# Layer 1's output projection folded into the seven-product scheme, as a third stream beside q and k

## The chip, the cores and the metric

The kernel runs on one core of one Trainium2 chip. The metric is the time of one execution on the device in microseconds (us), the median of several runs. The engines are called as in the profile: PE is the matrix engine (PEld its weight loads), ACT the scalar engine, DVE the vector engine, POOL the GpSimd engine, SP the engine that issues most transfers.

## What is computed

Two attention layers run one after the other over x of shape 1 x 128 x 256 x 256: 128 rows, each of 256 tokens with 256 channels, all float32. Each layer normalizes its input over groups of 8 channels, attends within every row, and adds its result to its input. Layer 1 is what the change is about:

```python
x2 = x.reshape(B * T, F, C)
qkv = x2 @ w_in.T + b_in
...
scores = jnp.einsum('bhid,bhjd->bhij', q, k) / jnp.sqrt(jnp.asarray(D, x.dtype))
keep = jnp.abs(i - j) <= band
scores = jnp.where(keep, scores, -jnp.inf)
attn = jax.nn.softmax(scores, axis=-1)
out = jnp.einsum('bhij,bhjd->bhid', attn, v)
y = out @ w_out.T + b_out
```

with 4 heads of 64 channels and a band of 16. Layer 0 has 8 heads of 32 channels, a bias added after its softmax, and a gate.

## The kernel before

Data lies channel by token: a row is a tile of 128 partitions by 2 halves of the channels by 256 tokens. A first stage (about 170 us) makes layer 0's bias and statistics, layer 0 follows, and layer 1 begins at about 2087 us. Between the layers x is kept in device memory (`x1`), and layer 1 reads it back two rows at a time into `yg` tiles (`load1`, five buffers).

A projection of two rows by a 256 x 256 weight is eight products of a 128 x 128 block of weights by 256 tokens (one row, one half of the channels in, one half out). Both layers' q and k, and layer 0's v and gate, are made by seven such products for a pair of rows instead of eight, by a Strassen-like scheme. `Quarters` holds sums of weight blocks, `row_sums` makes four sums `ts` of the pair's normalized input `xn` on POOL, and `Seven` issues products 1 to 7 (`product`), copies partial results out of the accumulator bank on ACT (`take`: "15" after products 1 and 5, "6", "7", and "34" at the end), and adds the pieces on POOL (`add`, lines 618 and 619). `sevens` runs two such projections f and g against each other. Product 2 of both goes into a bank of its own (`twos`), so that a pair of projections takes three accumulator banks.

The output projection of layer 1 (`project`, `one_by_one`, line 662) is plain: four products per row, eight per pair. `sevens` interleaves some of them as `po` between q's and k's products.

Layer 1's main loop takes one pair of rows per turn, and a hand-written order (`manual_schedule`) fixes what PE, ACT, DVE and POOL each do, in the order of the calls. For turn s (rows s and s+1), before the change:

- `scores` of both rows (PE line 997, then ACT's exponentials at 1005, then on POOL the mask product 1007 and the fold `zp` at 1014);
- `attend` for the two rows of the turn before (PE lines 1029 and 1039), `total` (ACT 1051, copies the denominators z out and sums them);
- `project(s - 4)`, then on DVE `inverse` (the reciprocal, line 1057) and `divide` (1063) for the two rows, with `finish(s - 4)` (bias and residual, 1081, and two transposes, 1095) between them, then `least` (1069);
- `stretch`: q and k for the next pair by `sevens`, with `project(s - 3)` between the products; `finish(s - 3)` and `store` to the output;
- `normal` for the pair after the next (ACT 940, then `row_sums` on POOL, 566 to 569), and `values` (PE 976, ACT 983) for the next pair.

The accumulator banks of layer 1 are a ring of four one-bank tiles, shared by scores, projections and values, and two tiles of two banks for `avz`.

Of the kernel before, what the change touches and what calls it, by code (L numbers as in the profile page):

```python
# [9 lines left out]
F32 = mybir.dt.float32  # L10
# [29 lines left out]
def conv_preact_kernel(  # L40
# [108 lines left out]

    NS = ("s1", "s2", "s3", "s4", "n11")

    class Quarters:

# [6 lines left out]
            return self.source[:, kt, self.col + m * P : self.col + (m + 1) * P]  # L162

        def sum(self):
            s1, s2, s3, s4, n11 = (self.sums[:, n, :] for n in range(len(NS)))
            w00, w10, w01, w11 = (self.quarter(kt, m) for m in range(2) for kt in range(2))
            nc.gpsimd.tensor_tensor(s1, w01, w11, ALU.add)
            nc.gpsimd.tensor_tensor(s2, s1, w00, ALU.subtract)
            nc.gpsimd.tensor_tensor(s3, w00, w01, ALU.subtract)
            nc.gpsimd.tensor_tensor(s4, w10, s2, ALU.subtract)  # L170
            nc.gpsimd.tensor_scalar(n11, w11, -1.0, None, op0=ALU.mult)

        def stationary(self, n):

            if n <= 2:
                return self.quarter(n - 1, 0)
            return self.sums[:, NS.index({3: "s4", 4: "n11", 5: "s1", 6: "s2", 7: "s3"}[n]), :]

    quarters = {w: Quarters(const, qkv_sb, n * C, w) for n, w in enumerate("qkv")}
    quarters["g"] = Quarters(const, gate_sb, 0, "g")  # L180
# [380 lines left out]
                )  # L561
        return ps

    def row_sums(t, x):

        nc.gpsimd.tensor_tensor(t[:, 0], x[:, 2], x[:, 0], ALU.subtract)
        nc.gpsimd.tensor_tensor(t[:, 1], x[:, 3], t[:, 0], ALU.subtract)
        nc.gpsimd.tensor_tensor(t[:, 2], x[:, 3], x[:, 2], ALU.subtract)
        nc.gpsimd.tensor_tensor(t[:, 3], t[:, 1], x[:, 1], ALU.subtract)

    class Seven:


        def __init__(self, pool, weights, x, t, name, tag, by_token=False, bias=None):
            self.weights, self.x, self.t, self.name, self.by_token, self.bias = weights, x, t, name, by_token, bias
            self.to = pool.tile([P, 4, R], F32, tag=tag, name=name, bufs=2)
            self.mid = pool.tile([P, 2, R], F32, tag="mid", name=f"mid{name}", bufs=2)

        def open(self):
            self.ps = proj_bank(f"p{self.name}")  # L580
# [21 lines left out]
                nc.scalar.activation(to, ps, AF.Identity, bias=self.bias[:, half : half + 1])  # L602

        def take(self, what):
            if what == "15":
                nc.scalar.copy(self.to[:, 0:4:3, :], self.ps)
            elif what == "6":
                self.copy(self.mid[:, 0, :], self.ps[:, 0, :], 0)
            elif what == "7":
                self.copy(self.mid[:, 1, :], self.ps[:, 0, :], 1)  # L610
            elif self.bias is None:
                nc.scalar.copy(self.to[:, 1:3, :], self.ps)
            else:
                self.copy(self.to[:, 1, :], self.ps[:, 0, :], 1)
                nc.scalar.copy(self.to[:, 2, :], self.ps[:, 1, :])  # L615

        def add(self, two):
            nc.gpsimd.tensor_tensor(self.to[:, 0], self.to[:, 0], two, ALU.add)  # L618
            nc.gpsimd.tensor_tensor(self.to[:, 2:4], self.to[:, 2:4], self.mid, ALU.add)  # L619

    def sevens(pool, f, g, name, po, rest=lambda: None):


        for p in (f, g):
            p.open()
            p.product(1)
            p.product(5)
            p.take("15")
            if p is f:
                rest()  # L630
        twos = proj_bank(f"p2{name}")
        two = pool.tile([P, 2, R], F32, tag="two", name=f"two{name}", bufs=2)
        f.product(2, twos[:, 0, :], first=True)
        g.product(2, twos[:, 1, :])
        if f.bias is None:
            nc.scalar.copy(two, twos)  # L636
        else:
            f.copy(two[:, 0, :], twos[:, 0, :], 0)
            g.copy(two[:, 1, :], twos[:, 1, :], 0)
        for p in (f, g):  # L640
            p.product(3)
            p.product(6)
            p.take("6")

        for n, what in ((7, "7"), (4, "34")):
            f.product(n)
            f.take(what)
            next(po, None)
            g.product(n)
            g.take(what)  # L650
        for _ in po:
            pass
        for n, p in enumerate((f, g)):
            p.add(two[:, n, :])

    def one_by_one(w, at, name, done):

# [19 lines left out]
    with ExitStack() as both:  # L677
        st1 = both.enter_context(tc.tile_pool(name="st1", bufs=1))

        stats1 = st1.tile([P, 2, S // 2 + 1, 6], F32, name="stats1")  # L680
        quarters1 = {w: Quarters(st1, w_in_t, n * C, f"1{w}") for n, w in enumerate("qk")}
        big1 = both.enter_context(tc.tile_pool(name="big1", bufs=2))
        ygs = {}

        def load1(g):
            if g * XG < S and g not in ygs:
                yg = big1.tile([P, XG, 2, R], F32, tag="yg", name=f"yg{g}", bufs=5)
                nc.sync.dma_start(out=yg, in_=rows(x1, g * XG, XG))
                ygs[g] = yg

        with ExitStack() as lay0:
# [27 lines left out]
            def sum_rows(i):  # L719
                if 2 * i < S:  # L720
                    tss[i] = row.tile([P, 4, R], F32, tag="ts", name=f"ts{i}", bufs=1)
                    row_sums(tss[i], xns[i])

            def scores(s, half):
                i, r = divmod(s, 2)
# [106 lines left out]
            def stretch(names, i, s, rest=lambda: None):  # L832

                po = iter(())
                if s >= 0:
                    po = one_by_one(out_sb, st[s]["at"], f"po{s}", lambda ps: st[s].update(po=ps))
                if 2 * i >= S:
                    rest()
                    for _ in po:
                        pass  # L840
                    return
                f, g = (
                    Seven(row, quarters[w], xns[i], tss[i], f"{w}{i}", w, by_token=(w == "v")) for w in names
                )
                for w, p in zip(names, (f, g)):
                    res[w, i] = p.to
                sevens(row, f, g, f"{names}{i}", po, rest)


            with tc.manual_schedule(engines={mybir.EngineType.PE, mybir.EngineType.Activation, mybir.EngineType.DVE}):  # L850
# [67 lines left out]
        with ExitStack() as lay:  # L918
# [10 lines left out]
            def normal(i, by_scalar):  # L929
# [13 lines left out]
                                x, y, mean1[:, col], rstd1[:, col], op0=ALU.subtract, op1=ALU.mult  # L943
                            )
                tss[i] = row.tile([P, 4, R], F32, tag="ts", name=f"1ts{i}", bufs=2)
                row_sums(tss[i], xns[i])

            def project(s):

# [1 line left out]
                    return iter(())  # L951
                return one_by_one(w_out_t, st[s]["at"], f"1po{s}", lambda ps: st[s].update(po=ps))

            def stretch(i, po):

                if 2 * i >= S:
                    for _ in po:
                        pass
                    return
                f, g = (  # L960
                    Seven(row, quarters1[w], xns[i], tss[i], f"1{w}{i}", w, bias=bqk[:, 0:2] if w == "q" else None)
                    for w in "qk"
                )
                sevens(row, f, g, f"1qk{i}", po)
                for r in range(2):
                    st[2 * i + r].update(q=f.to[:, 2 * r : 2 * r + 2, :], k=g.to[:, 2 * r : 2 * r + 2, :])

# [91 lines left out]
            def divide(s):  # L1059
                if s < 0:  # L1060
                    return
                at = row.tile([P, 2, R], F32, tag="at", name=f"1at{s}")
                nc.vector.tensor_tensor(at, hd.pop(s)[:, :, 0, :], st[s]["rz"], ALU.mult)
                st[s]["at"] = at

# [5 lines left out]
            def add(s, by_vector):  # L1071
# [1 line left out]
                if s < 0:  # L1073
                    return
                po, y = st[s]["po"], ygs[s // XG][:, s % XG]
                ot = row.tile([P, 2, R], F32, tag="ot", name=f"1ot{s}")
                st[s]["ot"] = ot
                for half in range(2):
                    b = bo_v[:, half : half + 1]
# [24 lines left out]
                    for a in range(A):  # L1104
                        nc.sync.dma_start(out=in_strips(out[0], s - 1, 2, a), in_=o[strip(a)])

            def finish(s):
                add(s, True)

            load1(0)  # L1110
            with tc.manual_schedule(engines={
# [6 lines left out]
                values(1)  # L1118
                normal(1, False)
                nc.vector.scalar_tensor_tensor(shift1, mean1, -1.0, rstd1, op0=ALU.mult, op1=ALU.mult)  # L1120
                stretch(0, iter(()))
                for s in range(0, S + 2, 2):
                    if s < S:
                        scores(s)
                        scores(s + 1)
# [1 line left out]
                    attend(s - 1)  # L1127
                    total(s - 2)
                    total(s - 1)
                    for _ in project(s - 4):  # L1130
                        pass
                    inverse(s - 2)
                    if s < S - 2:
                        finish(s - 4)
                    divide(s - 2)
                    inverse(s - 1)
                    divide(s - 1)
                    if s < S - 2:
                        least(s - 2)
                        least(s - 1)  # L1140
                        stretch(s // 2 + 1, project(s - 3))
                        finish(s - 3)
                        store(s - 3)
                        normal(s // 2 + 2, True)
                        values(s + 2)
                        values(s + 3)
                    else:

                        for _ in project(s - 3):
                            pass  # L1150
                        add(s - 4, False)
                        add(s - 3, False)
                for s in (S - 2, S - 1):
# [9 lines left out]

                for s in (S - 6, S - 5):
                    turn_row(s)
                finish(S - 1)
                for s in (S - 2, S - 4, S - 3):
                    turn_row(s)
                store(S - 1)
# [200 lines left out]
```

## Time and profile before

| | |
|---|---|
| median of 3 runs | 3215.15 us (3213.65 to 3216.70) |
| profiled execution, its own time | 3215.86 us |
| its span, first to last instruction | 3214.2 us |
| mean granted clock of PE | 0.991 |
| PE busy over the span | 3131.4 us (97%) |
| DVE, ACT, POOL busy | 2656.1, 2014.7, 1691.9 us |
| layer 1, 2200 to 3100 us: PE, DVE, ACT, POOL busy of 900 us | 898.5, 644.0, 582.2, 677.2 us |
| one turn of layer 1's loop, from one pair's reciprocal to the next (2599.83, 2616.88) | 17.05 us |

In the timeline a row gives the start, the time, the engine, the line, the operation, output and inputs, the shape and the count of merged instructions, and in brackets the idle time before it and who ended it. A 256-column product appears as two matmul records. A record's duration contains its way through the pipeline, so the pace is read from start to start.

### The profile page before, as it was taken

To read this page: it belongs to the slowest core of one execution; us is meant where nothing else is said; L and a number is where in the kernel's file an instruction comes from. 1 tells how busy PE (TensorE), PEld (TensorE's weight loads), DVE (VectorE), ACT (ScalarE), POOL (GpSimd) and SP (SyncE) were. 2 spreads that over 40 slices of the span, in tenths; PEclk is the share of its full clock that TensorE was granted. 3 is DMA by queue.
4 is the path that set the end of the run, shared out by engine and by line. 5 is a ranking of instruction groups with operands and counts; after the bars stand their busy time and mean duration, and the time that the engine had idled before them with its cause. 6 is when DMAs were issued, how large, how long until landed. Compare 5 with 4: busy or idle time off the path is not lost.

```text
span 3214.2 us, 86812 instructions
## 1 busy us (share of the span) xinstructions
PE 3131.4 (97%) x36965; PEld 2454.8 (76%) x36965; DVE 2656.1 (83%) x3507; ACT 2014.7 (63%) x4316; POOL 1691.9 (53%) x1660
## 2 busy tenths in 40 slices
PE   6789999999999999999999999999999999999997
PEld 4567777777777777777777777678888888888886
DVE  4669999999999999999999999847677777777776
ACT  4656666666666666666666666466666666666664
POOL 3034444444444444444444444286777777777775
PEclk8989999999999999999999999999999999999998
DMA  9931211111111111111111111012222222222222
GB/s 376 423 102 54 54 34 41 34 41 34 41 34 41 34 41 34 41 34 41 34 41 34 41 34 34 21 28 54 67 62 60 68 67 54 67 68 61 61 68 48
DMA packets 346187, 209.38 MB, mean 65 GB/s; under 512 B 273592, under 2 KB 339136, under 8 KB 339648
## 3 DMA queue, kind: packets, MB, share of 16 engines
q1 hardware_dynamic: 344896, 201.37, 21.7%
q8 instruction: 293, 4.80, 0.6%
q0 software_dynamic: 752, 2.36, 0.2%
q14 instruction: 102, 0.84, 0.1%
q10 hardware_dynamic: 144, 0.00, 0.0%
HBM read 136.59 MB, written 67.11 MB: 63 GB/s over the span
## 4 chain that ended last, share of the span: by engine, by line
PE 92%; DMA 4%; DVE 3%; POOL 0%; issue 0%; ACT 0%; SPq 0%; DVEq 0%; ACTq 0%; POOLq 0%
PE sim L731 8%; PE p1v L976 7%; PE 1po L662 7%; PE po L662 7%; PE av L763 7%; PE bv L763 7%; PE pv L595 6%; PE pq L591 6%; PE p1q L591 5%; PE pk L591 5%; PE pg L591 5%; PE p1k L591 5%; PE zs L777 4%; PE 1sim L997 3%; PE 1avz L1029 2%; DMA pr<-in_L_conv_pair_repr_dram 2%
## 5 line engine op out<-in xcount | busy, mean ns | idle before, releaser
L744 ACT ACTIVATE ex<-sim 128x512 f32<-128x512 f32 x1024 | 547.6, 605 | 429.6 <-PE sim L731 429.6
L1057 DVE RECIPROCAL 1rz<-1z 128x512 f32<-128x512 f32 x128 | 427.8, 3342 | 315.0 <-ACT 1z L1051 315.0
L753 DVE TENSOR_TENSOR both<-ex 128x512 f32<-128x512 f32 x512 | 483.5, 983 | 75.6 <-ACT ex L744 75.5
L793 DVE RECIPROCAL d<-d 128x512 f32<-128x512 f32 x128 | 429.2, 3353 | 4.4
L618 POOL TENSOR_TENSOR v<-v,twovg 128x256 f32<-128x256 f32 x64 | 74.8, 1168 | 548.2 <-ACT twovg L636 548.2
L731 PE MATMUL sim<-q,k 32*128 32x256 f32 x4096 | 295.6, 401 | 1.1 <-ACT ex L744 1.1
L662 PE MATMUL po<-at,out_sb 128*128 128x256 f32 x1024 | 284.9, 382 | 4.0 <-DVE at L811 4.0
L662 PE MATMUL 1po<-1at,w_out_t 128*128 128x256 f32 x1024 | 270.3, 388 | 1.2 <-ACT 1z L1051 1.1
L731 PEld LDWEIGHTS sim<-q,k 32*128 32x128 f32 x4096 | 186.4, 184 | 102.7 <-issue 94.2
L763 PE MATMUL bv<-bias_sb,v 128*32 128x256 f32 x4096 | 244.5, 379 | 0.7 <-DVE t L808 0.7
L763 PE MATMUL av<-ex,v 128*32 128x256 f32 x4096 | 244.5, 379 | 0.0
L1007 POOL TENSOR_TENSOR 1p<-1ex,seen 128x768 f32<-128x768 f32 x128 | 232.0, 1813 | 23.5 <-ACT 1ex L1005 23.5
L976 PEld LDWEIGHTS p1v<-w_in_t,1xn 128*64 128x64 f32 x4096 | 222.3, 137 | 21.5 <-issue 21.5
L976 PE MATMUL p1v<-w_in_t,1xn 128*64 128x128 f32 x4096 | 237.7, 274 | 0.3 <-PE warm L900 0.3
L662 PEld LDWEIGHTS 1po<-1at,w_out_t 128*128 128x128 f32 x1024 | 190.5, 191 | 50.6 <-ACT 1z L1051 23.1
L662 PEld LDWEIGHTS po<-at,out_sb 128*128 128x128 f32 x1024 | 185.6, 191 | 25.3 <-issue 4.3
L618 POOL TENSOR_TENSOR q<-q,twoqk 128x256 f32<-128x256 f32 x64 | 47.8, 748 | 297.3 <-ACT twoqk L636 297.3
L763 PEld LDWEIGHTS bv<-bias_sb,v 128*32 128x32 f32 x4096 | 133.2, 110 | 88.7 <-issue 1.1
L763 PEld LDWEIGHTS av<-ex,v 128*32 128x32 f32 x4096 | 133.2, 110 | 87.8 <-issue 0.3
L619 POOL TENSOR_TENSOR 1q<-1q,mid1q 128x512 f32<-128x512 f32 x64 | 81.6, 1275 | 189.3 <-ACT 1q L615 189.3
L713 DVE TENSOR_SCALAR xn<-xt,mean,rstd 128x256 f32<-128x256 f32 x256 | 180.0, 742 | 0.0
L1014 POOL TENSOR_TENSOR 1zp<-1p 128x512 f32<-128x512 f32 x128 | 162.6, 1270 | 10.0
(263 smaller groups left out, 7665.4 us busy)
## 6 DMA issues: line engine op xcount, KB each, us to landing
pr<-in_L_conv_pair_repr_dram SPq DMA_DIRECT2D x32, 1024.0 KB, 23.4
xs<-in_x_dram SPq DMA_DIRECT2D x16, 2048.0 KB, 23.4
x<-o SPq DMA_DIRECT2D x64, 512.0 KB, 3.0
yg<-x SPq DMA_DIRECT2D x64, 512.0 KB, 4.1
out_dram<-1o SPq DMA_DIRECT2D x256, 128.0 KB, 4.1
xg<-in_x_dram SPq DMA_DIRECT2D x252, 128.0 KB, 3.2
qkv_sb<-in_L_conv_qkv_proj_dram POOLq DMA_DIRECT2D x4, 192.0 KB, 13.9
w_raw<-in_L_conv_w_in_dram POOLq DMA_DIRECT2D x1, 768.0 KB, 13.2
```

Source lines behind the costliest of these rows:

```text
L591: nc.tensor.matmul(out, lhsT=weights, rhs=moving, start=first, **flags)
L595: nc.tensor.matmul(out[:, cols], lhsT=moving[:, cols], rhs=weights, start=first and t2 == 0, **flags)
L662: nc.tensor.matmul(ps[:, m, :], lhsT=w[:, kt, m * P : (m + 1) * P], rhs=at[:, kt, :], start=(kt == 0), stop=(kt == 1),)
L713: nc.vector.tensor_scalar(xns[i][:, 2 * r + half, :], xt[:, half, :], mean0[:, half : half + 1], rstd0[:, half : half + 1], op0=ALU.subtra ...
L731: nc.tensor.matmul(sims[j][:, kt, :], lhsT=k[p0 : p0 + D0, 2 * r + half, kt * P : (kt + 1) * P], rhs=q[p0 : p0 + D0, 2 * r + half, :], sta ...
L744: nc.scalar.activation(ex[:, j], sims[j], AF.Exp, scale=1.0 / math.sqrt(D0))
L753: nc.vector.tensor_tensor(both[:, j : j + 2], ex[:, j : j + 2, 0, :], ex[:, j : j + 2, 1, :], ALU.add)
L763: nc.tensor.matmul(to[D0 * j : D0 * (j + 1), half, :], lhsT=v[:, 2 * r + half, c0 : c0 + D0], rhs=weights(4 * half + j, kt), start=(kt == ...
L793: nc.vector.reciprocal(d, d)
L976: nc.tensor.matmul(ps[KB * half : KB * (half + 1), b, :], lhsT=xns[i][:, 2 * r + kt, KB * b : KB * (b + 1)], rhs=w_in_t[:, kt, 2 * C + P * ...
L1007: nc.gpsimd.tensor_tensor(p.rearrange("p j (r c) -> p (j r) c", c=WROW)[:, :, 0 : 2 * WSTEP] .rearrange("p r (t c) -> p r t c", c=WSTEP)[: ...
L1057: nc.vector.reciprocal(st[s]["rz"], st[s]["z"])
```

## The change

Products 1 to 7 are now issued for three projections in turn (`in_turn`): q and k of the next pair and the output projection "o" of an earlier pair. Product 2 no longer has a bank of its own: it is written first into the second half of the projection's bank, copied out (`take("2")`), and products 1 and 5 follow in the same bank. The attention output of both rows of a pair is one tile `ats`, and its four row sums `ats_t` are made on DVE. The pieces of "o" are added on POOL (`add_two`, `add_mid`); bias and residual (`finish`) then read the sum for both rows together, one turn later than before. `normal(i + 2)` stands at the head of a turn, ahead of `scores`. `yg` tiles live two turns longer, and two of every seven take layer 0's `xg` buffers. The sign of row sum 4 is turned, so that weight block w11 is used as it is and `n11` goes. The last rows are projected as before. Layer 0 keeps its order of work (`two_of_them`).

```diff
-    def row_sums(t, x):
-        nc.gpsimd.tensor_tensor(t[:, 0], x[:, 2], x[:, 0], ALU.subtract)
...
+    def row_sums(t, x, engine):
+        engine.tensor_tensor(t[:, 0], x[:, 2], x[:, 0], ALU.subtract)
+        engine.tensor_tensor(t[:, 1], x[:, 3], t[:, 0], ALU.subtract)
+        engine.tensor_tensor(t[:, 2], x[:, 3], x[:, 2], ALU.subtract)
+        engine.tensor_tensor(t[:, 3], x[:, 1], t[:, 1], ALU.subtract)
...
         def take(self, what):
-            if what == "15":
+            if what == "2":
+                self.copy(self.two, self.ps[:, 1, :], 0)
+            elif what == "15":
                 nc.scalar.copy(self.to[:, 0:4:3, :], self.ps)
...
+    def in_turn(pool, sevens):
+        for p in sevens:
+            p.open()
+            p.two = pool.tile([P, R], F32, tag=f"two{p.tag}", name=f"two{p.name}", bufs=1)
+            p.product(2, p.ps[:, 1, :], first=True)
+            p.take("2")
+        for p in sevens:
+            p.product(1)
+            p.product(5)
+            p.take("15")
+        for p in sevens:
+            p.product(3)
+            p.product(6)
+            p.take("6")
+        for n, what in ((7, "7"), (4, "34")):
+            for p in sevens:
+                p.product(n)
+                p.take(what)
+        for p in sevens:
+            p.add_two(p.two)
+        for p in sevens:
+            p.add_mid()
...
+                if g % 7 < 2:
+                    yg = big.tile([P, XG * (R // B), C // A], F32, tag="xg", name=f"yg{g}")
...
-            def finish(s):
-                add(s, True)
+            def finish(i):
+                if i < 0:
+                    return
+                ot = row.tile([P, 4, R], F32, tag="ot2", name=f"1ot2_{i}", bufs=1)
+                for half in range(2):
+                    nc.vector.scalar_tensor_tensor(
+                        ot[:, half::2, :], outputs[i].to[:, half::2, :], bo_v[:, half : half + 1], ygs[i][:, :, half, :],
+                        op0=ALU.add, op1=ALU.add,
+                    )
...
                 for s in range(0, S + 2, 2):
+                    i = s // 2
+                    bulk = s < S - 2
+                    if bulk:
+                        normal(i + 2, True)
                     if s < S:
                         scores(s)
                         scores(s + 1)
...
-                    for _ in project(s - 4):
-                        pass
-                    inverse(s - 2)
-                    if s < S - 2:
-                        finish(s - 4)
-                    divide(s - 2)
-                    inverse(s - 1)
-                    divide(s - 1)
-                    if s < S - 2:
+                    if s < S:
+                        finish(i - 3)
+                    for r in (s - 2, s - 1):
+                        inverse(r)
+                        divide(r)
+                    if bulk:
+                        if 0 <= i - 1 < S // 2 - 3:
+                            ats_t[i - 1] = row.tile([P, 4, R], F32, tag="att", name=f"1att{i - 1}", bufs=2)
+                            row_sums(ats_t[i - 1], ats[i - 1], nc.vector)
                         least(s - 2)
                         least(s - 1)
-                        stretch(s // 2 + 1, project(s - 3))
-                        finish(s - 3)
-                        store(s - 3)
-                        normal(s // 2 + 2, True)
+                        stretch(i + 1, i - 2)
                         values(s + 2)
                         values(s + 3)
```

## The prediction

> **What bounds the kernel now.** I read the shares of busy time first, then the busy time by stretch, then one turn of layer 1's loop in the timeline, engine by engine. The second line below is layer 1's steady part (columns: stretch, its length, then PE, PEld, DVE, ACT, POOL with counts, clock, transfers).
>
> ```profile
> PE 3131.4 (97%) x36965; PEld 2454.8 (76%) x36965; DVE 2656.1 (83%) x3507; ACT 2014.7 (63%) x4316; POOL 1691.9 (53%) x1660
> ...
> 2200.00:3100.00 900.00, 898.54 (x13296) 780.94 (x13293) 644.03 (x735) 582.15 (x1315) 677.17 (x633) 1.00 0.25 64
> ```
>
> PE is busy for 898.5 of 900 us at full clock, so in layer 1 PE alone sets the pace, and work taken from it counts in full until something else becomes late. What could become late is read from the turn's parts. PE:
>
> ```profile
> 2608.81 1.03 PE L662 MATMUL 1po<-1at,w_out_t 128*128 128x256 f32 x4
> 2609.77 3.71 PE L976 MATMUL p1v<-w_in_t,1xn 128*64 128x128 f32 x64
> 2613.41 1.56 PE L997 MATMUL 1sim<-1q,1k 64*64 64x96 f32 x61
> ...
> 2617.06 1.99 PE L662 MATMUL 1po<-1at,w_out_t 128*128 128x256 f32 x8
> 2618.89 0.59 PE L591 MATMUL p1q<-1xn,w_in_t 128*128 128x256 f32 x2
> 2619.32 0.59 PE L591 MATMUL p1q<-1ts,sums_1q 128*128 128x256 f32 x2
> ```
>
> From start to start: values 3.64 us, scores and attends 3.65 (2613.41 to 2617.06), one product 0.433 (two records, 2618.89 to 2619.32). The first four projections after the 64 x 64 work take 1.83, so about 0.1 goes in the switch. ACT over the same turn:
>
> ```profile
> 2609.50 2.08 ACT L940 ACTIVATE 1xn<-yg,shift,rstd 128x256 f32<-128x256 f32 x4
> 2611.78 0.59 ACT L983 COPY 1v<-p1v 128x512 f32<-128x512 f32 x1 [0.21 <-PE p1v L976]
> 2613.53 0.59 ACT L983 COPY 1v<-p1v 128x512 f32<-128x512 f32 x1 [1.16 <-PE p1v L976]
> 2614.41 1.64 ACT L1005 ACTIVATE 1ex<-1sim 128x384 f32<-128x384 f32 x4 [0.30 <-PE 1sim L997]
> 2616.16 0.60 ACT L1051 ACTIVATE 1z<-1avz 128x512 f32<-128x512 f32 x1
> 2616.65 0.19 ACT L1051 ACTIVATION_READ_ACCUMULATOR 1z<-1avz 128x1 f32 x1
> 2617.20 0.60 ACT L1051 ACTIVATE 1z<-1avz 128x512 f32<-128x512 f32 x1 [0.35 <-PE 1avz L1039]
> 2617.69 0.20 ACT L1051 ACTIVATION_READ_ACCUMULATOR 1z<-1avz 128x1 f32 x1
> 2619.96 0.59 ACT L606 COPY 1q<-p1q 128x512 f32<-128x512 f32 x1 [2.07 <-PE p1q L591]
> ```
>
> The reader is to see where ACT has room: the four normalizations run before the values' copies, while PE is in values, and after the second z ACT idles for 2.07 us until q's products come. ACT follows PE here; PE never waits for it. Two more facts: DVE's only idle time in a turn is 4.61 us before the first reciprocal, and POOL's is 0.33, 0.59 and 3.05 us.
>
> **What the Trainium skill says.** "PSUM — Partial Sum Buffer", section "PSUM bank collisions raise a hardware error", has kernels guard an accumulator bank as a whole: no engine may write one half while another reads the other. Before, product 2 had its own bank, so the trace has no such wait; in the changed program q's product 1, the next writer of q's bank, does wait for ACT, and product 5 does not. Section "Engine vs sequencer instructions" of that page calls ACT's queue strictly first in, first out; the rows above are in program order. "SBUF — State Buffer", section "SBUF: two separate sides", says that a DVE instruction with two SBUF inputs and a POOL instruction lock each other out. Layer 0's trace agrees:
>
> ```profile
> 1501.46 2.96 DVE L753 TENSOR_TENSOR both<-ex 128x512 f32<-128x512 f32 x3
> 1501.38 0.75 POOL L618 TENSOR_TENSOR q<-q,twoqk 128x256 f32<-128x256 f32 x1 [4.69 <-ACT twoqk L636]
> 1502.09 1.17 POOL L618 TENSOR_TENSOR k<-k,twoqk 128x256 f32<-128x256 f32 x1
> ```
>
> The POOL addition takes 0.75 us free and 1.17 with a DVE one beside it; the DVE ones take about 0.98 each, 0.68 where free (1509.23).
>
> **Part by part, per turn, time 0 being the first score on PE.**
>
> *Removed on PE*: one of 22 products, 0.433 us. It would make a turn 17.05 - 0.43 = 16.6.
>
> *Moved on ACT*: the normalizations now follow the second values' copy, and all that is behind them waits. That copy starts at 0.12 (2613.41 to 2613.53), and takes 0.49 (0.59 shown, 0.1 of it overlaps the next, as 2609.01 to 2609.50 for such a copy); four normalizations 1.99 (2609.50 to 2611.58, less the overlap); four exponentials 1.60; two z with their accumulator reads 2 x 0.68 = 1.36 (2616.16 to 2616.84). ACT is then at 5.56. The new copy of q's product 2 takes 0.47 with its bias (as mid1q), and PE goes on 0.12 later (the middle of 0.05 to 0.15 at the start of layer 1, where products waited for mid copies): **6.15**.
>
> *Order on PE*: with the plain projection gone from between, PE ends its attends at 3.65, and after the switch issues product 2 of q, k and o: 3.65 + 0.10 + 3 x 0.433 = 5.05. Product 1 of q waits from 5.05 to 6.15, **1.10 us idle**, and the other 17 products are queued behind it. Then 18 x 0.433 = 7.79, 0.10 for the switch and 3.64 of values: the next turn begins at 17.68, say **17.7**, against 17.05. A delay of the scores behind POOL by less than 1.1 us would not lengthen this, since the chain starts at the values' end. Within the 18 products nobody waits: three streams put at least two products (0.87 us) between a copy and its bank's next writer, and ACT's copies take 0.36 to 0.5 each.
>
> *ACT's other copies* for o add about 0.37 + 0.49 + 0.37 + 0.37 + 0.49 = 2.1 us; PE's 18 products and the values cover them.
>
> *POOL* before has 13.1 us of work a turn (17.05 less its idle 3.97); o adds 0.70 + 1.23 (the start-to-start of its additions at L618 and L619), so 15.0, and locks by DVE (two of 512 elements at 0.42, four of 256 at about 0.2, an estimate by halving) 1.6: 16.6, under 17.7. Its deadline is k's last addition before the next scores. Row sums start at 2.2 (third normalization), end at 5.0; masks and folds to 11.2; three add_two to 13.3; q's bank is copied at 14.1, so add_mid for q ends at 15.4 and for k at 16.7, with locks 17.2. Cover left: 0.5, and 1.1 more before PE's chain feels it.
>
> *DVE* before has 12.44 us (17.05 less 4.61). Two rows of bias, residual and transposes (1.72 each from 2610.47 to 2612.19) become two 512-element additions at 0.68 and four transposes at 0.37 (2.84), and four row sums add about 1.4: 13.2. The sum o of the turn before is complete at about 18, so its additions fall where POOL waits for normalizations and end well before z at 4.9. The row sums at 12.7 meet POOL's additions and wait for perhaps two, 1 to 2 us; DVE's idle time covers it.
>
> *Nothing*: the weight sums of o (four POOL operations in layer 0, against six n11 gone) lie in POOL's idle 8.7 us a row there. SP's loads and stores keep their number; yg has seven buffers for seven live pairs and is asked for a turn (17 us) ahead of a 4.1 us landing. Layer 0's product-2 tile with one buffer is free a row (14 us) before it is written again.
>
> *Ends*: turns 0 and 1 have no o and had no plain projection; turn 1 goes from 14.2 (2114.83 to 2129.02) to 6.15 + 12 x 0.433 + 0.1 + 3.64 = 15.1, and turn 0 has normalizations ahead of its exponentials: together +2. In the tail one more finish (2.8 us) goes ahead of the reciprocals, into DVE's idle 4.6.
>
> **Sum.** 61 turns with o at +0.65 is +40, and +2: 3215.86 + 42 = 3258 for the profiled execution. The median of the runs lies 0.7 lower: **3257**.
>
> **The rivals.** (a) *PE stays the bound*, one product shorter: 16.6 a turn, 61 x 0.43 = 26 less, 3189. This needs q's product-2 copy done by 5.05, 1.1 us earlier than I count; the sides change at 5.5, that is, if 0.65 us of ACT's six terms is not there. For it speaks that the exponentials before took 1.64 only as fast as scores came; against it that all terms but those are measured back to back. (b) *The SBUF lock makes DVE and POOL the bound.* If each of six two-input DVE instructions waits for a whole POOL one (15.0 us / 14 = 1.07 on average, 0.9 taken), DVE has 13.2 + 5.4 = 18.6 a turn: 61 x 1.55 = +95, 3310. Against it: POOL idles where two of them fall. (c) *A wash*: the two effects within 0.2% of each other (6.4 us, about what a measurement can tell from no change), 5.4 to 5.6 on the chain. (d) *The product isn't saved*, because a plain projection remains: only the last six rows keep it, so I give this no chance apart from (c).
>
> **How the numbers follow.** ACT's chain 0.70 (3238 to 3278, from 0.3 us either way on 6.15), the lock 0.16 (up to 3310), PE bound 0.09, a wash 0.05. So slower 0.86, same 0.05, faster 0.09. The range 3234 to 3288 takes in the chain and part of the lock's case.
>
> **What would show it.** After: a turn of 17.7 us; on PE a gap of about 1.1 us before the second product of q's bank, put down to ACT's copy of product 2; ACT without idle from the second values' copy to that copy; 42 products' records a turn at 0.217; DVE's wait for z still there, POOL's idle gone to about 1 us. It is wrong if PE stays gapless at 16.6, if PE waits before the scores for POOL's addition instead, or if ACT's 15-copy of o waits for DVE.

## The result and the profile after

| | before | after |
|---|---|---|
| median of the runs compared | 3214.0 us (3211.61 to 3216.70, 5 runs) | 3227.88 us (3227.81 to 3230.17, 5 runs) |
| profiled execution, its own time | 3215.86 us | 3227.81 us |
| its span | 3214.2 us | 3226.1 us |
| one turn of layer 1, steady | 17.05 us | 17.37 us |

The ratio after/before is 1.0044, 95% interval 1.0029 to 1.0059. The change makes the kernel slower, as forecast, but by 12 us (profiled executions) to 14 us (medians) where 42 were forecast; 3227.9 lies under the predicted range.

The shares of busy time of the kernel after, and below the dots its row for layer 1's steady part (columns as before):

```profile
PE 3117.8 (97%) x36843; PEld 2435.0 (75%) x36843; DVE 2938.5 (91%) x3629; ACT 2105.2 (65%) x4621; POOL 1876.1 (58%) x1780
...
2200.00:3100.00 900.00, 871.63 (x12919) 751.01 (x12913) 878.38 (x828) 651.45 (x1557) 825.76 (x727) 1.00 0.25 63
```

PE, busy 898.5 of 900 us before, now has 28 us idle in the same stretch: it no longer sets the pace. DVE is the busiest engine, and one could take it for the new bound; experiments below show that it is not. PE's rows of one turn in the timeline:

```profile
2615.39 1.56 PE L1036 MATMUL 1sim<-1q,1k 64*64 64x96 f32 x61
...
2619.03 0.70 PE L594 MATMUL p1q<-1xn,w_in_t 128*128 128x256 f32 x2
2619.57 0.59 PE L594 MATMUL p1k<-1xn,w_in_t 128*128 128x256 f32 x2
2620.00 0.59 PE L594 MATMUL p1o<-1at,w_out_t 128*128 128x256 f32 x2
2621.15 0.70 PE L594 MATMUL p1q<-1xn,w_in_t 128*128 128x256 f32 x2 [0.55 <-ACT two1q L605]
...
2632.76 1.56 PE L1036 MATMUL 1sim<-1q,1k 64*64 64x96 f32 x61
```

The gap stands where it was forecast: product 2 of q, k and o, then an idle PE until ACT has copied q's product 2. At 0.433 us a product PE would have gone on at 2620.43; it goes on at 2621.15, 5.76 us after the first score. From there to the next first score are 11.61 us. The list of waits (total, count, longest) has this one in nearly every turn, for the weight load (PEld) and for the matmul; no other wait of layer 1 holds a matmul in more than two turns:

```profile
PEld p1q L594 <- ACT two1q L605: 59.6, 64, 1.3
...
PE p1q L594 <- ACT two1q L605: 34.0, 62, 0.9
```

ACT over the same stretch, without an idle mark from the second values' copy on:

```profile
2615.50 0.58 ACT L1022 COPY 1v<-p1v 128x512 f32<-128x512 f32 x1 [1.16 <-PE p1v L1015]
2615.99 2.08 ACT L975 ACTIVATE 1xn<-yg,shift,rstd 128x256 f32<-128x256 f32 x4
2617.97 1.61 ACT L1044 ACTIVATE 1ex<-1sim 128x384 f32<-128x384 f32 x4
2619.45 0.61 ACT L1090 ACTIVATE 1z<-1avz 128x512 f32<-128x512 f32 x1
2619.92 0.23 ACT L1090 ACTIVATION_READ_ACCUMULATOR 1z<-1avz 128x1 f32 x1
2620.02 0.62 ACT L1090 ACTIVATE 1z<-1avz 128x512 f32<-128x512 f32 x1
2620.49 0.24 ACT L1090 ACTIVATION_READ_ACCUMULATOR 1z<-1avz 128x1 f32 x1
2620.59 0.51 ACT L605 ACTIVATE two1q<-p1q,bqk 128x256 f32<-128x256 f32 x1
```

From start to start: normalizations 1.98, exponentials 1.48, each z with its accumulator read 0.57, and 0.56 from the start of the copy to PE's next product.

The bank wait is what the Trainium skill, "PSUM — Partial Sum Buffer", section "PSUM bank collisions raise a hardware error", has a kernel keep: q's product 1 goes to the other half of the bank that ACT reads, and waits all the same.

### The profile page after: what moved, and what is told of

Its sections match the earlier page's. It is cut to its first block, busy times and chain, and to the rows that moved or that the text cites. A ratio compares the mean times of both kernels' runs of the same rounds, so it can differ in the third digit from the quotient of the medians.

```text
span 3226.1 us, 87360 instructions
## 1 busy us (share of the span) xinstructions
PE 3117.8 (97%) x36843; PEld 2435.0 (75%) x36843; DVE 2938.5 (91%) x3629; ACT 2105.2 (65%) x4621; POOL 1876.1 (58%) x1780
## 4 chain that ended last, share of the span: by engine, by line
PE 82%; ACT 9%; DMA 5%; issue 2%; DVE 2%; POOL 0%; SPq 0%; DVEq 0%; ACTq 0%; POOLq 0%
PE sim L766 8%; PE p1v L1015 7%; PE po L691 7%; PE av L798 7%; PE bv L798 7%; PE p1q L594 6%; PE pv L598 6%; PE pq L594 6%; PE pk L594 5%; PE p1k L594 5%; PE pg L594 5%; PE p1o L594 5%; DMA pr<-in_L_conv_pair_repr_dram 4%; PE zs L812 4%; ACT 1ex L1044 3%; ACT 1xn L975 3%
## 5 line engine op out<-in xcount | busy, mean ns | idle before, releaser
L1022 ACT COPY 1v<-p1v 128x512 f32<-128x512 f32 x128 | 75.0, 586 | 145.0 <-PE p1v L1015 145.0
L333 DVE BATCH_NORM_STATS2 stats<-xs 128x6 f32<-128x128 f32 x512 | 100.3, 276 | 63.9 <-DMA xs<-in_x_dram 63.9
L827 DVE SCALAR_TENSOR_TENSOR d<-g,z 128x512 f32<-128x512 f32 x128 | 113.1, 884 | 40.7 <-ACT z L825 40.5
```

## The experiments

The theory, A: ACT's chain from the values' end to the copy of product 2 sets the turn, one for one, because q's product 1 shares that copy's bank. The rivals: B, DVE (or DVE and POOL through their lock) sets it; and that the normalizations at the head cost by themselves.

**Normalizations back to the end of the turn.** `n_late` is the changed kernel with

```diff
-                    if bulk:
-                        normal(i + 2, True)
                     if s < S:
...
                         stretch(i + 1, i - 2)
+                        normal(i + 2, True)
                         values(s + 2)
```

> The changed kernel, but the four normalizations of the pair after the next (and their row sums on POOL) go back behind the three streams, ahead of the values, where they were before the change. Theory A (a turn is set by ACT's chain from the end of the values to the copy of q's product 2, which PE's next product in that bank waits for): the chain loses 1.98 us, PE no longer waits there, a turn is PE's own work, about 16.65 us against 17.37, and the whole about 3184 us. Theory B (DVE, which in the changed kernel's profile has hardly any idle time left because its two-input instructions wait for POOL's, sets the 17.37): DVE's work is the same, the turn stays at 17.2 to 17.4, the whole at 3218 to 3228.

Measured: 3184.78 us (ratio to before 0.9905, 0.989 to 0.992), turns of 16.61 us. Its row for the steady part:

```profile
2200.00:3100.00 900.00, 900.00 (x13515) 783.66 (x13514) 884.36 (x862) 705.95 (x1624) 872.13 (x759) 1.00 0.26 65
```

PE has no idle time left, with DVE still at 884 of 900. This is the seven-product saving as the prediction's first step counts it, 16.6 a turn.

**The copies ahead of the z.** `z_late` leaves the normalizations at the head and shortens the chain at its other end: `in_turn` becomes a generator that stops after the products 2 and their copies, and the main loop runs that part before `total`, with `finish` ahead of it:

```diff
                     attend(s - 1)
+                    if s < S:
+                        finish(i - 3)
+                    if bulk:
+                        work = stretch(i + 1, i - 2)
+                        next(work)
                     total(s - 2)
                     total(s - 1)
-                    if s < S:
-                        finish(i - 3)
...
-                        stretch(i + 1, i - 2)
+                        for _ in work:
+                            pass
```

> The changed kernel, but the three copies of product 2 on ACT come before the two copies of the denominators z, and not after them; all else is kept. Theory A: the chain to q's copy loses the two z, 1.14 us, more than the 0.7 us that PE waits, so a turn becomes 16.65 us and the whole about 3184 us. Theory B: z comes to DVE later by three copies (1.0 us), DVE has nothing to spare, the turn stays at 17.4 or grows; 3228 or more.

Measured: 3185.87 us (0.9908, 0.9893 to 0.9923), turns of 16.58 to 16.59. ACT and PE in its timeline:

```profile
2612.04 2.08 ACT L976 ACTIVATE 1xn<-yg,shift,rstd 128x256 f32<-128x256 f32 x4
2614.03 1.60 ACT L1049 ACTIVATE 1ex<-1sim 128x384 f32<-128x384 f32 x4
2615.09 0.70 PE L594 MATMUL p1q<-1xn,w_in_t 128*128 128x256 f32 x2
2615.89 0.48 ACT L605 ACTIVATE two1q<-p1q,bqk 128x256 f32<-128x256 f32 x1 [0.26 <-PE p1q L594]
...
2616.49 0.63 PE L594 MATMUL p1q<-1xn,w_in_t 128*128 128x256 f32 x2
```

The normalizations stand where the change put them, and cost nothing once the copy follows the exponentials: ACT now waits 0.26 us for PE. The times of `n_late` and `z_late` can't be told apart, and both beat the kernels before and after.

**One normalization of four.** `n_one` moves the last one only, with POOL's row sums that need it (`normal` is given the numbers of the normalizations that it makes):

```diff
-                        normal(i + 2, True)
+                        normal(i + 2, True, (0, 1, 2))
...
                         stretch(i + 1, i - 2)
+                        normal(i + 2, True, (3,))
                         values(s + 2)
```

> The changed kernel, with the last of the four normalizations (and POOL's row sums, which need it) moved back from the head of the turn to ahead of the values; three normalizations stay at the head. Theory A (ACT's chain sets the turn, one for one): the chain is shorter by one normalization, 0.50 us, and still longer than PE's way to product 2: a turn of 17.37 - 0.50 = 16.87 us, PE's wait for the copy of product 2 down from 0.55 to about 0.1 to 0.25 us, total 3228 - 61 x 0.50 = 3197.5 (3195 to 3200). Rival (a threshold: what costs is POOL's row sums at the head, which need all four normalizations and meet DVE there): 16.6 us a turn and 3184 to 3187, the whole gain with one of four moved.

Measured: 3202.91 us (0.9957, 0.9944 to 0.9971), turns of 16.91. The chain in its timeline, on a turn whose first score is at 2605.06:

```profile
2605.65 1.58 ACT L978 ACTIVATE 1xn<-yg,shift,rstd 128x256 f32<-128x256 f32 x3
...
2609.76 0.51 ACT L605 ACTIVATE two1q<-p1q,bqk 128x256 f32<-128x256 f32 x1
...
2610.32 0.70 PE L594 MATMUL p1q<-1xn,w_in_t 128*128 128x256 f32 x2
```

PE goes on at 5.26 us, 0.50 earlier than after the change (5.76), and the turn is 0.46 shorter: nearly one for one, and no threshold at the row sums. The total missed its range by 3 us: 61 turns at 0.46 are 28, not 30.5, and layer 1's first values come 1.9 us later than after the change (2088.70 against 2086.79) and its first turn is 1.0 longer. In that turn PE's granted clock was 0.66 from 2102 to 2107 us, against 1.00 after the change, which is a likely cause of the 1.0; the 1.9 stays without one.

**DVE without the row sums.** `no_att` is the changed kernel with

```diff
-                            ats_t[i - 1] = row.tile([P, 4, R], F32, tag="att", name=f"1att{i - 1}", bufs=2)
-                            row_sums(ats_t[i - 1], ats[i - 1], nc.vector)
+                            if i - 1 < 2:
+                                ats_t[i - 1] = row.tile([P, 4, R], F32, name=f"1att{i - 1}", bufs=1)
+                                row_sums(ats_t[i - 1], ats[i - 1], nc.vector)
+                            else:
+                                ats_t[i - 1] = ats_t[(i - 1) % 2]
```

and `n_late_no_att` is `n_late` with the same. Both leave out the row sums from the third pair on, so their output is not layer 1's.

> The changed kernel with the four row sums of the attention output made on DVE for the first two pairs only; all later pairs use those again (the output is then not layer 1's). DVE has 4.8 us less of work and waits in a turn, POOL meets four two-input instructions fewer. Theory A: nothing changes on ACT's chain, the turn stays at 17.37 us and the whole at 3228; DVE idles some 4 us ahead of the first reciprocal. Theory B: the turn falls clearly below 17.37, to between 16.65 and 17.0, the whole to 3184 to 3205.

> The changed kernel with the four normalizations back ahead of the values, and DVE's row sums of the attention's output made for the first two pairs of rows only and reused (so layer 1's output is not the reference's). Theory A (with the normalizations back, PE is the bound and DVE, busy 884 of 900 us, only waits inside its instructions): the turn stays 16.6 us, the total 3183 to 3187, DVE's busy time down by 4 to 6 us a turn. Rival (DVE is the next bound and holds the turn at 16.6 as well as PE): a turn below 16.55, total under 3180.

Measured: `no_att` 3229.17 us (1.0041, 1.0028 to 1.0055), turns of 17.36 and 17.37 still; `n_late_no_att` 3182.61 (0.9895, 0.988 to 0.991), turns of 16.61 and 16.62. The steady part of the first, then of the second:

```profile
2200.00:3100.00 900.00, 871.65 (x12954) 751.08 (x12948) 619.67 (x624) 651.56 (x1557) 761.99 (x726) 1.00 0.26 63
```

```profile
2200.00:3100.00 900.00, 900.00 (x13515) 783.61 (x13514) 691.05 (x649) 707.14 (x1626) 838.68 (x758) 1.00 0.26 66
```

DVE loses 258.7 of its 878.4 us (5.0 us a turn) and the turn does not move. In the second, DVE falls from 884 to 691, and the turn stays too. Rival B falls in both places: DVE at 98% was not the bound.

**The move alone, in the kernel before.** `b_head` is before with the normalizations at the head of the turn:

```diff
                 for s in range(0, S + 2, 2):
+                    if s < S - 2:
+                        normal(s // 2 + 2, True)
                     if s < S:
...
                         store(s - 3)
-                        normal(s // 2 + 2, True)
```

> The kernel before with the one move alone: the normalizations stand at the head of a turn, ahead of the scores; product 2 keeps its own bank and the output projection its eight products. Theory A: it takes the move and the shared bank together to make PE wait. Here PE has 1.83 us of plain projection between attends and q's products, and q's bank is first read only after products 1 and 5, so ACT's 2 us of delay are covered: a turn stays at 17.05 us, the whole within 0.2% of before. If the move alone delays PE (by the scores' banks, which ACT frees 1.3 us later): up to 17.4 a turn, 3235 us.

Measured: 3423.43 us (1.0652, 1.0637 to 1.0666), which neither theory expected. Its waits show why:

```profile
ACT 1xn L940 <- DMA yg<-x: 199.5, 59, 6.2
PEld 1po L662 <- ACT 1ex L1005: 184.5, 60, 5.9
PE 1po L662 <- ACT 1ex L1005: 157.4, 57, 5.4
```

ACT waits up to 6.2 us for `yg`, everything behind it on ACT is late, and PE waits for the exponentials. Before has five `yg` buffers. `normal` asks for the next pair's load when it is called, and that load needs the buffer that `finish(s - 3)` frees late in the same turn; with `normal` at the head the load lands after the next head: in the turn whose first score is at 2601.79 us the load is issued at 2602.13, and ACT starts to normalize at 2606.27, after 3.78 us idle. The two buffers that the change takes from layer 0's pool are what lets it move the normalizations. `b_head7` adds them to `b_head`:

```diff
-                yg = big1.tile([P, XG, 2, R], F32, tag="yg", name=f"yg{g}", bufs=5)
+                if g % 7 < 2:
+                    yg = big.tile([P, XG * (R // B), C // A], F32, tag="xg", name=f"yg{g}")
+                    yg = yg.rearrange("p n c -> p (n c)").rearrange("p (s h q) -> p s h q", h=2, q=R)
+                else:
+                    yg = big1.tile([P, XG, 2, R], F32, tag="yg", name=f"yg{g}", bufs=5)
```

> The kernel before, with the normalizations moved to the head of the turn as in the changed kernel, and with the changed kernel's load1 (seven buffers of yg for five). Plain projections and the two-product scheme with product 2 in a bank of its own stay. Theory A (the move costs only because q's product 1 shares a bank with ACT's copy of product 2, which stands at the end of ACT's chain): no PE wait, PE gapless, a turn of 17.05 us, total 3207 to 3217, no measurable change; and the 6.2 us waits for yg that the same move with five buffers showed are gone. Theory B (the move alone delays PE, by late exponentials or late row sums): turns of 17.3 us or more, 3230 or more.

Measured: 3214.28 us (0.9997, 0.9989 to 1.0005), turns of 17.01 and 17.02 but for some longer ones (see below), none of the waits for `yg`; from 2250 to 2850 us PE is busy for all 600. ACT in its timeline:

```profile
2607.92 2.08 ACT L944 ACTIVATE 1xn<-yg,shift,rstd 128x256 f32<-128x256 f32 x4
2609.90 1.60 ACT L1009 ACTIVATE 1ex<-1sim 128x384 f32<-128x384 f32 x4
...
2613.86 0.59 ACT L606 COPY 1q<-p1q 128x512 f32<-128x512 f32 x1 [1.20 <-PE p1q L591]
```

The same 1.98 us of normalizations ahead of the exponentials cost nothing here: ACT still waits 1.20 us for q's products, since no product waits for a copy that stands behind z. So neither the move nor the shared bank costs alone. It is the two together: a copy that PE waits for, at the end of a lengthened chain. One thing stays open: `b_head7` differs from the change in more than the bank, since it also keeps 1.83 us of plain projection between the attends and q's products. The change with product 2 in a bank of its own was not run.

**The long early turns.** In the trace of before, measured from one first values' matmul to the next, turns 3 to 11 of layer 1 (the first is 0) are not 17.05 us but 18.50, 18.27, 18.27, 17.92, 18.18, 17.48, 17.30, 17.13, 17.27, and only then 17.05, with two short relapses: in all 7.0 us more than with 17.05 each. Six of them show a gap on PE; the first four are put down to "issue":

```profile
2150.57 0.66 PE L1039 MATMUL 1avz<-1zp,ones 64*64 64x256 f32 x8 [1.21 <-issue]
2168.85 0.66 PE L1039 MATMUL 1avz<-1zp,ones 64*64 64x256 f32 x6 [0.68 <-issue]
2187.12 0.65 PE L1039 MATMUL 1avz<-1zp,ones 64*64 64x256 f32 x4 [0.57 <-issue]
2205.05 0.64 PE L1039 MATMUL 1avz<-1zp,ones 64*64 64x256 f32 x2 [0.24 <-issue]
```

"Issue" means that the profile shows nothing that PE waited for. The place moves by two matmuls a turn, which speaks against data. The other two stand on line 662: 1.05 us in turn 7, put down to ACT's z, and 0.17 in turn 8. After has no such turn: from turn 2 on all are 17.36 or 17.37, but for a last one of 16.58. `b_shift` is before with four matmuls more, ahead of the loop:

```diff
+                extra = proj_bank("extra")
+                for _ in range(4):
+                    nc.tensor.matmul(extra[:, 0, :], lhsT=ident, rhs=out_sb[:, 0, :], start=True, stop=True)
                 for s in range(0, S + 2, 2):
```

> The kernel before, with four matmuls of 128x256 more on PE (products that nobody reads), ahead of turn 0's scores in layer 1, where PE waits 2.9 us for POOL: eight records more in PE's stream, and nothing else. Theory P (the gaps of 1.2 to 0.2 us on PE in turns 3 to 12 of layer 1, which the profile puts down to issue, belong to a place in PE's stream of instructions): the gaps move to other matmuls or turns, or change in number; the sum of the turns' excess over 17.05 changes from its 7 us, and the total falls in 3207 to 3217. Theory Q (they belong to these turns' data): the same turns keep the same lengths (18.5, 18.3, 18.3, 17.9, 18.2, 17.5, 17.3) with gaps on the same matmuls of L1039 within two records, total as before within 0.05%.

Measured: 3219.74 us (1.0012, 1.0005 to 1.0018), turns of 18.70, 18.30, 18.30, 18.04, 18.73, 18.28, 18.27, 18.26, 18.18, 17.48, 17.60. Its gaps:

```profile
2149.00 0.37 PE L1029 MATMUL 1avz<-1p,1v 64*64 64x80 f32 x8 [1.41 <-issue]
2167.31 0.29 PE L1029 MATMUL 1avz<-1p,1v 64*64 64x80 f32 x3 [1.01 <-issue]
...
2222.52 0.66 PE L1039 MATMUL 1avz<-1zp,ones 64*64 64x256 f32 x8 [1.46 <-issue]
```

Eight records more in PE's stream put the first gaps on another line, and the long turns last to turn 13 and not to 11: the excess is 12.8 us for 7.0. Theory P holds, by its number and place of gaps; its total, which I had put at 3217 at most, is off, since I had not thought that there could be more of them. They belong to the place in PE's stream, not to the turns' data. Nor are they bound to the layer's start: six of turns 2 to 8 of `b_head7` are long, and so are its turns 46 to 50 (17.48 to 18.40), 7.5 us in all.

## Why the prediction was right or wrong

**Right: the mechanism and its sign.** The saved product (16.6 a turn where PE is the bound: 16.61 in `n_late`), PE ready after three products 2 (5.05 forecast; 2620.43 - 2615.39 = 5.04), the wait for ACT's copy, and PE's part after it (11.53 forecast, 11.61 measured, the first product after the wait taking 0.1 longer) came as worked out.

**Wrong: the length of ACT's chain, 6.15 us forecast and 5.76 measured.** Term by term:

| term | forecast | measured |
|---|---|---|
| second values' copy, start and length | 0.12 + 0.49 | 0.11 + 0.49 |
| four normalizations | 1.99 | 1.98 |
| four exponentials | 1.60 | 1.48 |
| two z with accumulator reads | 1.36 | 1.14 |
| copy of product 2, and PE going on | 0.47 + 0.12 | 0.56 |

The mis-sized terms are two, with the same mistake: a length was read to the end of a record, where the next instruction had already begun. For z I took 0.68, from the start of one z to the end of its read (2616.16 to 2616.84); but the next instruction starts 0.13 us before that read ends (2620.02 against 2619.92 + 0.23), so back to back it is 0.57. For the four exponentials I took 1.60, from a row of 1.64. After the change, where they wait for no score, that row still takes 1.61, but the first z starts 1.48 after the first exponential. So the doubt under rival (a), that the exponentials before went only as fast as scores came, was worth 0.03 us at most; and its counter, that all other terms had been measured back to back, was wrong for z. Together the two are 0.34 of 0.39 us, and 0.39 is more than the 0.3 that the range allowed on the chain. As PE's wait is the difference of two large numbers, an error of 6% in the chain took the step from +0.65 to +0.32 a turn: 61 x 0.32 = 19.5 us for 40.

**Wrong: "61 turns with o at +0.65", which took 17.05 us for every turn before.** The 7.0 us of long early turns were in the trace of before; the prediction read one turn in the middle. Between the first scores of turns 2 and 63 (2129.02 and 3175.96 before, 2129.14 and 3187.70 after) the difference is 11.6 us: 19.5, less 7.0, less 0.8 for a last turn of 16.58. That accounts for the 11.95 between the two profiled executions, with +0.1 ahead and +0.2 in the tail, where "ends together +2" had been forecast. So some 7 us of the result come from these long turns and not from the chain: by what `b_shift` shows, another stream of matmuls could have kept them or added more. The clock plays into the +0.1 too: from 2102 to 2107 us, in turn 0, PE's granted clock was 0.68 before and 1.00 after, and from first score to first score turn 0 takes 14.12 us before against 12.58 in `b_shift`, where it was 1.00. At equal clocks the ends would have been nearer to the forecast +2 (an estimate: 1.5 us more).

**The rivals.** (a) *PE bound* needed the copy at 5.05, and this condition was stated rightly: the chain was 0.72 us too long for it, and `n_one` (5.26) and `n_late` walk across that point. Its 3189 is 4 us over `n_late`, which loses the early turns' excess as well. (b) *The lock*: its first half is true. DVE's row sums after:

```profile
2612.14 0.42 DVE L567 TENSOR_TENSOR 1att<-1at 128x256 f32<-128x256 f32 x1
2612.60 1.38 DVE L568 TENSOR_TENSOR 1att<-1at,1att 128x256 f32<-128x256 f32 x1
2613.90 1.50 DVE L569 TENSOR_TENSOR 1att<-1at 128x256 f32<-128x256 f32 x1
2615.32 1.50 DVE L570 TENSOR_TENSOR 1att<-1at,1att 128x256 f32<-128x256 f32 x1
```

0.42 us free and 1.4 to 1.5 where POOL's additions of 128x512 run beside them (2612.22, 2613.66, 2615.07 on POOL), so 4.8 us for the 1.4 that I had put down, and DVE busy for 878 of 900 us where the prediction had 13.2 of 17.7 and 1 to 2 of lock. But these waits shrink when there is less time: in `n_late` the same four take 3.4 us (0.65, 0.84, 0.95, 0.95). It never decided. One sign failed here: "DVE's wait for z still there". Before, DVE waits 4.61 us a turn for z; after, it does so only 6 times from 2200 to 3100 us, 6.5 us in all.

**POOL.** The cover of 0.5 us before the scores was 0.27: k's last addition ends at 2615.12 (2613.66 and 1.46), the first score is at 2615.39. PE never waited for it.

## What to carry to other kernels

Where a change makes two engines wait for each other in turn, the new turn is the longer of two chains; write each as starts, not as durations, because the end of an instruction's record can overlap the next one, and here an error of 6% in a chain was half of the difference. Here the wait cost only where two things met: a copy that guards an accumulator bank, and its place behind everything that the same engine was given first; taking either away gave back the whole saving. Before pricing one turn times the number of turns, measure the length of every turn.

## What the runs showed of the hardware

**An engine busy for 98% need not be near the bound.** DVE's time in the steady part was 878 us with a turn of 17.37 and 884 of 900 with one of 16.61, and 691 at 16.61 once the row sums were gone. The Trainium skill, "SBUF — State Buffer", section "SBUF: two separate sides", calls the pair of SBUF ports that DVE and POOL share an exclusive lock, held for a whole instruction; the rows above agree (1.38 to 1.50 us behind a POOL addition, 0.42 where DVE came first), and add that the wait is counted as DVE's busy time. A busy share alone does not tell such waiting from work; taking the row sums away did.

**Gaps of PE put down to "issue" seem to go with its instruction fetch.** The transfers of before in a half microsecond ahead of the first gap (queue, kind: packets, MB, share of 16 engines; the packets' times are added up, and can pass 100%):

```profile
q1 hardware_dynamic: 495, 0.14, 119.0%
q8 instruction: 1, 0.02, 12.3%
```

Queue q8 brings instructions: in the page of before 293 packets and 4.80 MB, 16.4 KB each, or 65 bytes for each of the 2 x 36965 records of PE and PEld, so it seems to be PE's. "Runtime: NRT & Kernel Launch", section "Terms", of the same skill has the instruction memory refilled in 16 KiB blocks, which agrees. In turns with a gap a packet of q8 starts 5.1 to 6.3 us after the values' start, and PE goes on 1.2 to 1.6 us after the packet's end: at 1.37, 1.45, 1.38 and 1.44 in the four gaps shown of before, and 1.21 to 1.57 in the eleven of `b_shift`. This fits a late fetch. But the packet's place in the turn does not make a gap by itself: in `n_late` one starts 5.0 to 6.2 us after the values' start in each of turns 7 to 33, and PE, busy without a pause, shows none. That the gaps hang on the place in the stream is shown; that a late fetch causes them is not, and that the transfers beside it delay it was not tried.
